# A two-layer transformer on one core: GpSimd in written order, side work at fixed places of a step, head biases picked on chip, routing moved two steps forward

## The chip, the cores and the metric

The kernel runs on one core of one Trainium2 chip. A core has TensorE (PE; its weight loads are shown as PEld), VectorE (DVE), ScalarE (ACT), GpSimd (POOL) and SyncE (SP), which issues most of the DMAs. The metric is the device time of one execution in microseconds (us), the median of several runs. All times below come from one profiled execution unless a median is named.

## The reference, cut to what matters

x is 2 x 1024 x 256 (two batches, 16 tiles of 128 tokens in all), the context 2 x 77 x 256, all in f32. Four sub-layers follow one another; each normalizes the rows (LN) and adds its result to x.

```python
x = x + xattn(LN(x), ctx, ctx, mask, Wq, bq, Wk, bk, Wv, bv, Wo, bo)  # 16 heads of 16, 77 keys
x = x + heads(LN(x), Wq, bq, Wk, bk, Wv, bv, Wr, br, Wo, bo)          # 4 of 16 heads of 64, 1024 keys
x = x + einsum(gelu(einsum(LN(x), ctx)), ctx)                         # 77 context rows as a hidden layer
x = x + moe(LN(x), w_router, w1, b1, w2, b2)                          # top 1 of 8 experts, hidden 1024

def heads(y, ...):
    dist = softmax(mean(y @ Wr + br, axis=1))       # one choice for a whole batch
    idx  = sort(top_k(dist, 4))
    Q, K, V = the idx heads of y @ Wq + bq, y @ Wk + bk, y @ Wv + bv
    return softmax(Q @ K.T / 8) @ V, heads side by side, @ Wo + bo
```

So the second attention can't project anything until the mean over all 1024 tokens of its batch is known, and the experts need the router's choice for every token.

## The kernel before

The program has three phases.

**Phase a**, steps a0 to a19, one tile of 128 tokens a step, software-pipelined: step s makes the scores of tile s (`a_scores`), transposes the weights of tile s-1 (`a_transposed`), forms the weights of tile s (`a_weights`: row maximum and subtraction on DVE, exponential on ACT), multiplies tile s-2 with the values (`a_values`; `rc` and `hn` normalize it on DVE), turns tile s-3 and projects tile s-4 (`a_projected`, which adds to `xs`, the residual stream in SBUF). Before step a0 stand the turned weights of q and k, the keys (`context_k`, laid out by head in `kblk`) and the first queries. The values are spread over heads by `context_v` and `place_v`.

**Phase b**, steps b0 to b36, is the second attention. An item is one tile with two of the four heads, 32 items. Step s makes the scores of item s (`b_scores`, tile `bsc`), transposes the weights of item s-1 in four groups of four (`b_transposed(j, h, k0)`, tiles `bpt` to `beT`), takes row maxima and exponentials of item s (`b_weights`, `bnm` and `be`), multiplies item s-3 with v (`b_values`, `bov`), and every second step forms the reciprocal sums, turns them (`b_inverse_sums`, `b_turned_sums`: `brb`, `brt`, `brT`) and normalizes (`b_normalized`, `boT`). `b_projected` (`po_b`) adds to `xs`.

**Phase e**, from about 500 us, sorts tokens by expert and runs 20 blocks of 128 tokens through the experts' weights; the change does not touch it.

Work that belongs to other sub-layers is hung on these steps as side pieces:

- `do_rows(tag, t0)` normalizes the rows of two tiles: statistics on DVE, the power -1/2 and the two rows `y` on POOL (on DVE for the last two tiles of c and d), then on POOL the next output bias into `xs`. `do_turn` transposes them on PE and ACT copies them to `yT`. The tag is a for the first attention, b for the second, c for the context layer, d for the experts' router.
- `route_sums`, `route_logits`, `route_heads` choose the four heads of a batch; `route_heads` then has SP read each head's number and load its slices of Wk, Wq, Wv and of the biases. `b_qk` projects q and k, `b_v` the values.
- `c_hidden`, `c_out`, `d_logits`, `d_expert` are the context layer and the router for two tiles; groups g = 0 to 7 follow four steps apart.

The order of the work is written by hand for PE, DVE and ACT: these three run their instructions as the program text lists them. POOL's order was left to the framework's scheduler. `at(stage, s, f, ...)` hangs a piece on a step and `take` runs the pieces after the step's own work; only one projection a step goes in the middle (`project`). The weights of the chosen heads have one buffer each, so those of batch 1 wait for the projections of batch 0. PSUM is split into three pools: `big` (scores, two tiles of two banks), `trp` (transposes, two banks) and `accp` (accumulation, two banks).

Of the kernel before, what the change touches and what calls it, by code (L numbers as in the profile page):

```python
# [39 lines left out]
def kernel(  # L40
# [127 lines left out]
    nc.sync.dma_start(wrt_s, w_router.rearrange("(c p) e -> p c e", p=P))  # L168
    b1r = const.tile([E * FC, P], F32, name="b1r")
# [176 lines left out]
    def context_k(m, eng):  # L346
        ps = accp.tile([P, B, KC], F32, name=f"kps_{m}", tag="acc")
        for c in range(C):
            nc.tensor.matmul(
                ps.rearrange("p b k -> p (b k)"),  # L350
                lhsT=wT["k"][:, c, m * P : (m + 1) * P],
                rhs=ctxT[:, c].rearrange("p b k -> p (b k)"),
                start=(c == 0),
                stop=(c == C - 1),
            )
        kT = small.tile([P, B, KC], F32, name=f"kT_{m}", tag="kT")
        nc.vector.scalar_tensor_tensor(kT, ps, bk_c[:, m : m + 1], keep01, ALU.add, ALU.mult)
        for j in range(HG):
            eng.tensor_scalar(kblk[:, :, m, j, :], kT, hmask[:, j : j + 1], None, ALU.mult)
# [10 lines left out]

    def context_v(b):
        ps = accp.tile([KC, D], F32, name=f"vcps_{b}", tag="acc")
# [4 lines left out]
        nc.vector.tensor_tensor(vc[:, b, :], ps, bv_b[:KC, :], ALU.add)  # L377

    def place_v(g):
        ps = accp.tile([P, half, B, HW, HD], F32, name=f"vps_{g}", tag="acc")  # L380
        for i in range(half):
# [3 lines left out]
                ps[:, i].rearrange("p b h d -> p b (h d)"),  # L385
# [3 lines left out]
            )  # L389
        gs = slice(g * half, (g + 1) * half)  # L390
# [94 lines left out]
    def a_step(s):  # L485

        scs = a_scores(s) if s < T else None
        if 0 <= s - 1 < T:
            a_transposed(s - 1, 0, nc.scalar.copy)
            a_transposed(s - 1, 4, nc.scalar.copy)  # L490
        if s < T:
            a_weights(s, scs)
        if 0 <= s - 2 < T:
            a_values(s - 2)
# [5 lines left out]
        if 0 <= s - 4 < T:  # L500
            a_projected(s - 4)

# [4 lines left out]
    def route_sums(b, n):  # L507

        if b not in sel:
            sel[b] = small.tile([P, 2, C], F32, name=f"ys_{b}", tag="ysum")  # L510
        nc.vector.tensor_reduce(
            sel[b][:, n // 512, :], yTs["b", b][:, :, n : n + 512], AX.X, ALU.add
        )

    def route_logits(b):
        ys = sel[b]
        ym = small.tile([P, C, P], F32, name=f"ym_{b}", tag="ym")
        nc.vector.tensor_tensor(ys[:, 0, :], ys[:, 0, :], ys[:, 1, :], ALU.add)
        nc.vector.tensor_scalar(
            ym, ys[:, 0, :].unsqueeze(2).to_broadcast([P, C, P]), 1.0 / S, None, ALU.mult  # L520
        )
        ps = sel[b] = accp.tile([P, NH], F32, name=f"rps_{b}", tag="acc")
# [10 lines left out]
    def route_heads(b):  # L533
# [31 lines left out]
        bc = {k: wsp.tile([P, NP], F32, name=f"bc_{k}{b}", tag=f"bc_{k}") for k in "qk"}  # L565
        bv = wsp.tile([P, NA, FD], F32, name=f"bvs_{b}", tag="bvs")
        for s in range(NA):
            h = nc.values_load(seli[0:1, s : s + 1], engines=SP, min_val=0, max_val=NH - 1)
            for k, src in (("k", f_wk), ("q", f_wq), ("v", f_wv)):
                v = src.rearrange("(c p) (h d) -> p c h d", p=P, h=NH)  # L570
                nc.sync.dma_start(w[k][:, :, s : s + 1, :], v[:, :, bass.ds(h, 1), :])
            with nc.allow_non_contiguous_dma(reason="bias columns"):
                for k, src in (("k", f_bk), ("q", f_bq)):
                    v = src.rearrange("(h d) -> d h", h=NH)
                    r = slice((s % 2) * FD, (s % 2) * FD + FD)
                    nc.sync.dma_start(bc[k][r, s // 2 : s // 2 + 1], v[:, bass.ds(h, 1)])
            v = f_bv.rearrange("(h d) -> h d", h=NH)
            nc.sync.dma_start(bv[:, s, :], v[bass.ds(h, 1), :].to_broadcast([P, FD]))

        bqs = wsp.tile([P, NP], F32, name=f"bqs_{b}", tag="bqs")  # L580
        nc.gpsimd.tensor_scalar(bqs, bc["q"], float(FD) ** -0.5, None, ALU.mult)
        sel[b] = w, {"k": bc["k"], "q": bqs}, bv
# [133 lines left out]
    def b_step(s, project=None):  # L716

# [3 lines left out]
        sc = b_scores(i) if i < NI else None  # L721
        if 0 <= j < NI:
# [5 lines left out]
        if project is not None:  # L728
            b_qk(*project)()
# [8 lines left out]
        if 0 <= k < NI:  # L738
            if k % TG == 0:
                b_turned_sums(k // TG)  # L740
            else:
                b_normalized(k // TG)
        i = s - PR
        if 0 <= i < NI and split(i)[2] == NP - 1:
            b_projected(i)

# [3 lines left out]
    def c_hidden(t0):  # L750

# [3 lines left out]
        for c in range(C):  # L755
            nc.tensor.matmul(
                ps, lhsT=ctxT[:, c, b, :], rhs=yT[:, c, :], start=(c == 0), stop=(c == C - 1)
            )
        g = gs[t0] = ap_.tile([KC, 2 * P], F32, name=f"g_{t0}", tag="g")
# [30 lines left out]
    TE2 = [P, 2, E]  # L790

    def d_logits(t0):
        yT = yTs.pop(("d", t0))
        ps = trp.tile([P, 2, E], F32, name=f"elps_{t0}", tag="tr")
# [6 lines left out]
        nc.vector.tensor_copy(logits[:, t0 : t0 + 2, :], ps)  # L801

    def d_expert(t0):

        ts_ = slice(t0, t0 + 2)
        lg, hot = logits[:, ts_, :], oh[:, ts_, :]
# [28 lines left out]
    def at(stage, s, f, *args):  # L835
        plan.setdefault((stage, s), []).append((f, args))

    def take(stage, s):
        for f, args in plan.pop((stage, s), []):
# [21 lines left out]
    at("a", 0, turn_weight, "v")  # L861
    for b in range(B):
        at("a", 0, context_v, b)
    at("a", 0, do_rows, "a", 4, bo_b)
    at("a", 0, do_rows, "a", 6, bo_b)
    at("a", 0, add_bias, 0, 4, bo_b)
    for g in range(2):
        at("a", 1, place_v, g)
    at("a", 1, do_turn, "a", 4)
    at("a", 1, do_turn, "a", 6)  # L870
    at("a", 1, do_rows, "a", 8, bo_b)
    at("a", 2, query, 0, 512, 0)
    at("a", 2, query, 0, 512, 1)
    at("a", 3, turn_weight, "o")
    at("a", 3, do_turn, "a", 8)
    at("a", 3, do_rows, "a", 10, bo_b)
    at("a", 4, do_turn, "a", 10)
    at("a", 4, do_rows, "a", 12, bo_b)
    at("a", 5, do_turn, "a", 12)
    at("a", 5, query, 1, 0, 0)  # L880
    at("a", 6, query, 1, 0, 1)
    at("a", 6, do_rows, "a", 14, bo_b)
    at("a", 7, do_turn, "a", 14)
    at("a", 8, query, 1, 512, 0)
    at("a", 9, query, 1, 512, 1)
    at("a", 10, expert_biases)

    for i in range(4):
        at("a", 2 * i + 6, do_rows, "b", 2 * i, fbo_b)
        at("a", 2 * i + 7, do_turn, "b", 2 * i)  # L890
    at("a", 10, route_sums, 0, 0)
    at("a", 14, route_sums, 0, 512)
    at("a", 14, route_logits, 0)
    at("a", 15, route_heads, 0)
    for args in ((0, "k", 0, 0), (0, "k", 0, 512)):
        at("a", 17, do_qk, *args)
    at("a", 18, do_qk, 0, "q", 0, 0)
    for s, args in ((0, (0, "k", 1, 0)), (0, (0, "k", 1, 512)), (1, (0, "q", 1, 0))):
        at("b", s, do_qk, *args)
    for t in range(NT):  # L900
        at("b", (0, 0, 1, 1, 2, 2, 3, 3)[t], b_v, 0, t)

    for i in range(4):
        s = 2 * i + 14
        stage, s = ("a", s) if s < 19 else ("b", s - 19)
        at(stage, s, do_rows, "b", NT + 2 * i, fbo_b)
        s = 2 * i + 15
        stage, s = ("a", s) if s < 19 else ("b", s - 19)
        at(stage, s, do_turn, "b", NT + 2 * i)
    at("b", 0, route_sums, 1, 0)  # L910
    at("b", 3, route_sums, 1, 512)
    at("b", 3, route_logits, 1)
    at("b", 4, route_heads, 1)
    project = {4: (0, "q", 0, 512), 5: (0, "q", 1, 512)}
    for s, args in enumerate(
        (("k", 0, 0), ("k", 0, 512), ("q", 0, 0), ("k", 1, 0), ("k", 1, 512), ("q", 1, 0),
         ("q", 0, 512), ("q", 1, 512))
    ):
        project[s + 7] = (1, *args)
    for t in range(NT):  # L920
        at("b", 10 + t, b_v, 1, t)

    for g in range(T // TG):
        s, t0 = 4 * g, TG * g
        at("b", s + 8, do_rows, "c", t0, None, None, g == T // TG - 1)
        at("b", s + 10, do_turn, "c", t0, accp, "acc")
        at("b", s + 12, c_hidden, t0)
        at("b", s + 13, c_out, t0)
        at("b", s + 13, do_rows, "d", t0, None, ztok, g == T // TG - 1)
        at("b", s + 14, do_turn, "d", t0, accp, "acc")  # L930
        at("b", s + 16, d_logits, t0)
        at("b", s + 16, d_expert, t0)
    at("b", 30, d_probability, 0, NT)

    with tc.manual_schedule(
        engines={mybir.EngineType.PE, mybir.EngineType.DVE, mybir.EngineType.Activation}
# [15 lines left out]
        rows["a", 0], rows["a", 2] = ys[:2], ys[2:]  # L952
        for b in range(B):
# [8 lines left out]
        context_k(0, nc.vector)  # L962
        context_k(1, nc.gpsimd)
        for j in range(HG):
            nc.vector.tensor_scalar(
                mneg[:, :, j, :], mask_i, 0.0, neg3, ALU.is_equal, ALU.mult
            )
        query(0, 0, 0)
        query(0, 0, 1)
        for s in range(T + 2):  # L970
            a_step(s)
            take("a", s)
# [3 lines left out]
        take("a", T + 2)  # L976
        for s in range(NI + PR):
            b_step(s, project.get(s))
# [232 lines left out]
```

## Time and profile before

| | |
|---|---|
| median of 3 runs | 679.14 us (676.03 to 679.31) |
| profiled execution | 681.69 us, of which its span 679.9 us |
| busy in the span | PE 592.3 (87%), PEld 430.8 (63%), DVE 340.1 (50%), ACT 236.5 (35%), POOL 172.4 (25%) |
| mean granted TensorE clock | 0.93 |
| moved by DMA | 62.72 MB, most of it the experts' weights after 500 us |

The page is read so: busy time counts an engine's instructions, and matmul ends are modelled. The slices cut the span in 40 parts of 17 us; a digit is the busy share in tenths, and PEclk is the TensorE clock that was granted. A list of waits says which instruction of which engine stood idle, what released it, the total, how often and the longest. A group's line has its line in the program, engine, operation, the tile written and those read, shapes and count, then busy time and the mean of one. The scores of step a2 begin at 40.42 us in this execution, those of b0 at 173.25, and the last product with v ends at 460.27.

### The profile page before, as it was taken

How to read it: one execution, taken by the hardware profiler on the slowest of the kernel's cores; microseconds unless marked ns; L12 is line 12 of the kernel's file. 1: busy time of each engine (PE TensorE's matmuls, PEld its weight loads, DVE VectorE, ACT ScalarE, POOL GpSimd, SP SyncE). 2: the span in 40 equal slices, each digit the busy share in tenths (PEclk: the TensorE clock that was granted, in tenths of full speed). 3: DMA queues.
4: the chain of work that ended last, by engine and by line, in shares of the span. 5: the costliest groups of instructions: out<-in, count | busy, mean ns of one | idle time of the engine just before them, and what ended most of it. 6: DMA issues, size and time to landing. Idle time of an engine off the chain costs nothing. (4 is left out here: it accounts for less than half of the span.)

```text
span 679.9 us, 9956 instructions
## 1 busy us (share of the span) xinstructions
PE 592.3 (87%) x3661; PEld 430.8 (63%) x3661; DVE 340.1 (50%) x824; ACT 236.5 (35%) x473; POOL 172.4 (25%) x218
## 2 busy tenths in 40 slices
PE   6689999987888999999999999995444999999995
PEld 3368777875454555565655566563334999899884
DVE  4457666752355655464767675763360332332331
ACT  3235454531244444434444645531100211111110
POOL 3363352223120002021222130303122122323121
PEclk9679999969798999999999999998555999999999
DMA  8000000002000100000000000000129499999990
GB/s 241 1 1 1 1 1 1 1 1 53 3 0 1 39 17 1 1 16 16 1 32 16 16 21 11 33 1 31 47 101 358 175 341 353 361 354 373 331 321 15
DMA packets 50824, 62.72 MB, mean 92 GB/s; under 512 B 12664, under 2 KB 43859, under 8 KB 50773
## 3 DMA queue, kind: packets, MB, share of 16 engines
q1 hardware_dynamic: 47504, 54.03, 23.7%
q0 software_dynamic: 2560, 7.34, 3.0%
q10 hardware_dynamic: 709, 0.68, 0.3%
q8 instruction: 30, 0.49, 0.3%
q14 instruction: 21, 0.17, 0.1%
HBM read 55.75 MB, written 6.82 MB: 92 GB/s over the span
## 5 line engine op out<-in xcount | busy, mean ns | idle before, releaser
L654 DVE TENSOR_REDUCE bnm<-bsc 128x1 f32<-128x1024 f32 x64 | 75.3, 1219 | 45.0 <-PE bsc L640 45.0
L666 PEld LDWEIGHTS bpt<-ident,be 128*128 128x128 f32 x512 | 54.8, 141 | 43.6 <-issue 20.4
L656 ACT ACTIVATE be<-bsc,bnm 128x1024 f32<-128x1024 f32 x64 | 70.8, 1110 | 17.1 <-DVE bnm L654 16.1
L666 PE MATMUL bpt<-ident,be 128*128 128x128 f32 x512 | 71.4, 280 | 5.8 <-DVE beT L667 5.3
L1131 PE MATMUL ph<-ybT,w1s 128*128 128x128 f32 x640 | 76.3, 278 | 0.0
L1131 PEld LDWEIGHTS ph<-ybT,w1s 128*128 128x128 f32 x640 | 74.5, 195 | 2.6 <-DVE ybT L1126 2.2
L1148 PE MATMUL epo<-w2s,ehT 128*128 128x256 f32 x320 | 75.2, 379 | 0.0
L1137 ACT ACTIVATE ehT<-ph,b1s 128x128 f32<-128x128 f32 x80 | 22.9, 369 | 144.8 <-issue 105.7
L640 PE MATMUL bsc<-kT,qT 64*128 64x512 f32 x256 | 67.1, 644 | 5.8 <-ACT qT L598 5.8
L667 ACT COPY beT<-bpt 128x512 f32<-128x512 f32 x64 | 37.5, 586 | 95.8 <-PE bpt L666 94.8
L1139 DVE TENSOR_SCALAR ehT<-ph,b1s 128x128 f32<-128x128 f32 x80 | 22.5, 345 | 93.8 <-ACT ehT L1137 88.9
L676 PE MATMUL bov<-beT,v 128*64 128x256 f32 x512 | 62.3, 385 | 0.0
L1148 PEld LDWEIGHTS epo<-w2s,ehT 128*128 128x128 f32 x320 | 57.9, 190 | 6.3
L667 DVE COPY beT<-bpt 128x512 f32<-128x512 f32 x64 | 43.4, 686 | 29.3 <-PE bpt L666 29.2
L676 PEld LDWEIGHTS bov<-beT,v 128*64 128x64 f32 x512 | 33.9, 136 | 25.5 <-issue 7.4
L688 POOL COPY brb<-brc 128x256 f32<-128x256 f32 x16 | 6.4, 400 | 153.6 <-DVE brc L686 150.4
L640 PEld LDWEIGHTS bsc<-kT,qT 64*128 64x128 f32 x256 | 23.0, 194 | 31.0 <-issue 21.9
L1157 POOL DMA_INDIRECT out_dram<-ob,etok x20 | 20.2, 1012 | 82.5 <-DMA out_dram<-ob,etok 70.0
L456 PE MATMUL av<-vblk,eT 128*128 128x51 f32 x320 | 39.6, 282 | 0.0
L456 PEld LDWEIGHTS av<-vblk,eT 128*128 128x128 f32 x320 | 39.6, 202 | 0.1
L432 DVE TENSOR_REDUCE mx<-sc 128x8 f32<-128x616 f32 x32 | 25.4, 794 | 26.3 <-PE sc L418 26.3
L448 ACT COPY eT<-pt 128x512 f32<-128x512 f32 (+1 forms) x48 | 23.3, 514 | 38.1 <-PE pt L447 37.5
(227 smaller groups left out, 849.7 us busy)
## 6 DMA issues: line engine op xcount, KB each, us to landing
w1s<-in_L_ffn_w_dram SPq DMA_DIRECT2D x20, 1024.0 KB
w2s<-in_L_ffn_w_dram SPq DMA_DIRECT2D x20, 1024.0 KB
b2s<-in_L_ffn_b_dram SPq DMA_DIRECT2D x20, 128.0 KB
xs<-in_x_dram SPq DMA_DIRECT2D x4, 512.0 KB
ztok<-xs SPq DMA_DIRECT2D x16, 128.0 KB
ztok<-y_d SPq DMA_DIRECT2D x16, 128.0 KB
ws_k<-in_L_ffn_Wk_dram SPq DMA_DIRECT2D x8, 64.0 KB
ws_q<-in_L_ffn_Wq_dram SPq DMA_DIRECT2D x8, 64.0 KB
```

The source lines that it names most:

```text
L432: nc.vector.tensor_reduce(mx, scv, AX.X, ALU.max)
L448: copy(eTs[t][:, c0 : c0 + n, :], pt[:, :n, :])
L456: nc.tensor.matmul(av[:, h0 : h0 + HW, :].rearrange("p h d -> p (h d)"), lhsT=eT[:, c, :], rhs=vblk[:, t // NT, c].rearrange("p h d -> p ( ...
L640: nc.tensor.matmul(sc[h][:, n : n + 512], lhsT=qks[b, "q", m][r, q0 : q0 + P], rhs=qks[b, "k", m][r, n : n + 512], start=True, stop=True,)
L654: nc.vector.tensor_reduce(nm, sc[h], AX.X, ALU.max, negate=True)
L656: nc.scalar.activation(bes[i][:, h], sc[h], AF.Exp, bias=nm, accum_out=sms[g][:, q, s : s + 1])
L666: nc.tensor.transpose(pt[:, k - k0, :], bes[i][:, h, k * P : (k + 1) * P], ident)
L667: copy(beTs[gm][:, h, k0 : k0 + 4, q * P : (q + 1) * P], pt)
L676: nc.tensor.matmul(ovs[gm][h * FD : (h + 1) * FD, :], lhsT=vs[g * TG // NT][:, k, 2 * m + h, :], rhs=beTs[gm][:, h, k, :], start=(k == 0), ...
L1131: nc.tensor.matmul(ph[:, f, :], lhsT=ws[n][0][:, c, f * P : (f + 1) * P], rhs=ybT[:, c, :], start=(c == 0), stop=(c == C - 1),)
L1137: nc.scalar.activation(hT[:, f, :], ph[:, f, :], AF.Relu, bias=b1s[:, f : f + 1])
L1148: nc.tensor.matmul(po, lhsT=hT[:, f, :], rhs=w2s[:, f, :], start=(f == 0), stop=(f == FC - 1))
```

## The change

- POOL's instructions also run in written order. The second half of `kblk` is formed on DVE, not POOL. Rows 4 to 7 of phase a are normalized ahead of the context's transposes, W_v is turned ahead of step a0, and the bias of tiles 0 to 7 is one piece at the end of a0.
- `at` and `take` get a position inside a step: 0 after the scores, 1 (phase a) after the weights, 2 (phase b) after the first two groups of transposes, 3 at the end. Producers in PSUM and their readers are split (`context_v` and `context_v_bias`, `place_v` and `place_v_heads`, `c_hidden` and `c_gelu`; `d_logits` leaves its copy to `d_expert` and uses `accp`). The turned sums go from the end of the odd step to just behind the scores of the next step.
- The biases of all 16 heads of q and k are loaded once, turned on PE (`head_biases`), and the chosen ones are picked on DVE with a one-hot product. The loads of columns and the small POOL operation on q's bias are gone. SP loads k and q slices first, then v, then v's biases.
- The routing of batch 0 sums two tiles at a time, forms its mean in a13 and its heads in the middle of a14 (before: a14 and the end of a15). The projections start at the end of a15 (before: a17). Batch 1 has logits and heads in b3 (before: b3 and b4).
- The context layer and router of group g run from 4g+8 to 4g+13 instead of 4g+8 to 4g+16.

```diff
+    hbr = const.tile([2 * NH, 2, FD], F32, name="hbr")
+    for i, ap in enumerate((f_bk, f_bq)):
+        for j in range(2):
+            nc.sync.dma_start(hbr[i * NH : (i + 1) * NH, j, :], ap.rearrange("(h d) -> h d", h=NH))
...
         for j in range(HG):
-            eng.tensor_scalar(kblk[:, :, m, j, :], kT, hmask[:, j : j + 1], None, ALU.mult)
+            nc.vector.tensor_scalar(kblk[:, :, m, j, :], kT, hmask[:, j : j + 1], None, ALU.mult)
...
+    def head_biases():
+
+        ps = trp.tile([P, 2 * NH], F32, name="hbps", tag="tr")
+        nc.tensor.transpose(ps, hbr.rearrange("p j d -> p (j d)"), ident[: 2 * NH, : 2 * NH])
+        nc.scalar.copy(hbT[:, 0, :], ps[:, :NH])
+        nc.scalar.activation(hbT[:, 1, :], ps[:, NH:], AF.Copy, scale=float(FD) ** -0.5)
...
+    def route_mean(b):
+        ys = small.tile([P, C], F32, name=f"yt_{b}", tag="yt")
+        nc.vector.tensor_reduce(ys, sel[b], AX.X, ALU.add)
+        ym = sel[b] = small.tile([P, C, P], F32, name=f"ym_{b}", tag="ym", bufs=1)
+        nc.vector.tensor_scalar(
+            ym, ys.unsqueeze(2).to_broadcast([P, C, P]), 1.0 / S, None, ALU.mult
+        )
...
+        load(0, "k", "q")
+        load(1, "k", "q")
+        load(2, "k")
+        load(3, "k", "q")
+        load(2, "q")
         for s in range(NA):
-            h = nc.values_load(seli[0:1, s : s + 1], engines=SP, min_val=0, max_val=NH - 1)
-            for k, src in (("k", f_wk), ("q", f_wq), ("v", f_wv)):
...
-                    nc.sync.dma_start(bc[k][r, s // 2 : s // 2 + 1], v[:, bass.ds(h, 1)])
...
-        nc.gpsimd.tensor_scalar(bqs, bc["q"], float(FD) ** -0.5, None, ALU.mult)
+            load(s, "v")
...
+        hot = small.tile([P, NA, NH], F32, name=f"hot_{b}", tag="hot", bufs=1)
+        nc.vector.tensor_tensor(
+            hot, iota16.unsqueeze(1).to_broadcast([P, NA, NH]),
+            se.unsqueeze(2).to_broadcast([P, NA, NH]), ALU.is_equal,
+        )
+        hb = small.tile([P, 2, NA, NH], F32, name=f"hb_{b}", tag="hb", bufs=1)
+        nc.vector.tensor_tensor(
+            hb, hot.unsqueeze(1).to_broadcast([P, 2, NA, NH]),
+            hbT.unsqueeze(2).to_broadcast([P, 2, NA, NH]), ALU.mult,
+        )
...
         sc = b_scores(i) if i < NI else None
+        take("b", s, 0)
+        if 0 <= k < NI and k % TG == TG - 1:
+            b_turned_sums(k // TG)
         if 0 <= j < NI:
             b_transposed(j, 0, 0, nc.scalar.copy)
         if i < NI:
             b_weights(i, sc)
         if 0 <= j < NI:
             b_transposed(j, 0, 4, nc.vector.tensor_copy)
-        if project is not None:
-            b_qk(*project)()
+        take("b", s, 2)
...
-        if 0 <= k < NI:
-            if k % TG == 0:
-                b_turned_sums(k // TG)
-            else:
-                b_normalized(k // TG)
+        if 0 <= k < NI and k % TG == TG - 1:
+            b_normalized(k // TG)
         i = s - PR
         if 0 <= i < NI and split(i)[2] == NP - 1:
             b_projected(i)
+        take("b", s, 3)
...
+    at("a", 0, 3, add_bias, 0, 8, bo_b)
...
+    at("a", 13, 3, route_logits, 0)
+    at("a", 14, 1, route_heads, 0)
+    at("b", 3, 2, route_logits, 1)
+    at("b", 3, 3, route_heads, 1)
...
     for t in range(NT):
-        at("b", 10 + t, b_v, 1, t)
+        at("b", 8 + t, 0, b_v, 1, t)
...
-        at("b", s + 8, do_rows, "c", t0, None, None, g == T // TG - 1)
-        at("b", s + 10, do_turn, "c", t0, accp, "acc")
-        at("b", s + 12, c_hidden, t0)
-        at("b", s + 13, c_out, t0)
-        at("b", s + 13, do_rows, "d", t0, None, ztok, g == T // TG - 1)
-        at("b", s + 14, do_turn, "d", t0, accp, "acc")
-        at("b", s + 16, d_logits, t0)
-        at("b", s + 16, d_expert, t0)
-    at("b", 30, d_probability, 0, NT)
+        at("b", s + 8, 3, do_rows, "c", t0, None, None, last)
+        at("b", s + 10, 0, do_turn, "c", t0)
+        at("b", s + 10, 2, c_hidden, t0)
+        at("b", s + 10, 3, c_gelu, t0)
+        at("b", s + 11, 2, c_out, t0)
+        at("b", s + 11, 3, do_rows, "d", t0, None, ztok, last)
+        at("b", s + 12, 2, do_turn, "d", t0, accp, "acc")
+        at("b", s + 13, 2, d_logits, t0)
+        at("b", s + 13, 3, d_expert, t0)
+    at("b", 30, 3, d_probability, 0, NT)
...
-        context_k(0, nc.vector)
-        context_k(1, nc.gpsimd)
+        context_k(0)
...
+        context_k(1)
         query(0, 0, 0)
         query(0, 0, 1)
+        turn_weight("v")
         for s in range(T + 2):
             a_step(s)
```

In the last loop s stands for 4g and t0 for 2g; the same loop of before has no positions.

## Prediction

> **What bounds the kernel now.** I read the page's slices first, then TensorE's waits, the windows with their clocks, and the timeline at each long wait.
>
> ```profile
> PE   6689999987888999999999999995444999999995
> ...
> PEclk9679999969798999999999999998555999999999
> ```
> A slice is 17 us. TensorE (PE) is full in the middle of both attentions and in the experts (527 us to the end). It has holes at the start, around slices 8 to 12, and at the seam (slices 27 to 30); the clock dips in the same places.
>
> ```profile
> PE bsc L640 <- ACT qT L598: 5.8, 1, 5.8
> ...
> PE sc L409 <- POOL kblk L359: 4.5, 1, 4.5
> PE lps_a L306 <- POOL y_a L283: 2.4, 2, 1.7
> PE bpt L666 <- DVE beT L667: 2.3, 2, 1.2
> PE rps L524 <- issue: 2.2, 1, 2.2
> PE rps L524 <- DVE ym L519: 2.2, 1, 2.2
> PE vcps L374 <- ACT wvT L337: 1.9, 1, 1.9
> PE bps_k L591 <- DMA ws_k<-in_L_ffn_Wk_dram: 1.5, 1, 1.5
> ```
> TensorE's waits up to 222 us (total, times, longest): single events, nearly all at a step that the change moves.
>
> ```profile
> 21.80:32.00 10.20, 8.29 (x28) 4.47 (x30) 3.81 (x10) 1.19 (x2) 0.10 (x1) 0.50 0.00 1
> ...
> 38.80:45.70 6.90, 6.18 (x28) 4.12 (x27) 3.40 (x5) 1.58 (x3) 6.59 (x6) 0.51 0.00 1
> ...
> 141.30:151.50 10.20, 10.20 (x47) 9.53 (x44) 5.26 (x15) 3.76 (x7) 4.42 (x4) 0.50 0.01 2
> ...
> 172.00:178.80 6.80, 5.55 (x12) 2.70 (x13) 1.73 (x2) 1.16 (x2) 0.48 (x2) 0.50 0.01 2
> ...
> 222.00:440.00 218.00, 208.85 (x1296) 126.28 (x1295) 135.43 (x265) 108.92 (x198) 40.05 (x47) 1.00 0.06 17
> ```
> Windows: length, busy time of PE, PEld, DVE, ACT, POOL, then the granted clock. After each long wait the clock is halved for 7 to 10 us, so a wait costs itself and half the busy time that follows. 222 to 440 us (the body of the second attention) is full: 9.15 us idle in 218.
>
> The Trainium skill ("TensorE: Matmul & The Clock Gate", "Why this matters for your kernels") asks only that idle gaps stay below about 3 us. The trace disagrees: after a gap of 2.21 us (at 139.35) the window from 141.3 is at 0.50. By the page, the short gaps below would cost no clock and the sum would be some 7 us smaller.
>
> **The change, part by part** (gains positive, us).
>
> *Start, +13.* POOL first adds bo_b (16.72 to 19.05, having waited for the load), only then forms half of kblk (4 operations, 2.67), for which PE waits 4.5. On DVE the like four took 0.93, and DVE's queue becomes: y_a to 10.15, row statistics of four more tiles (2.45, as at 30.45 to 32.9), keep01 0.23, kT and kblk 1.3, mneg 0.92, kT and kblk 1.3: ready at 16.4. PE ends the queries at 16.4 and now turns W_v there (1.1), so the first scores begin near 17.5 and end near 19; the v projection follows without its 1.9 wait (3.70 at half clock, some 1.9 at full). DVE ends step 0's weights and the v bias at 22.4, place_v (2.4) then runs to 24.8, the transposes of e to 26.4, two turned blocks to 28. Their rows are ready, since POOL makes them from 11.4 to 17.7, ahead of the 4.7 us of bias adds (eight tiles in one; nothing needs those before step 4). Step 2's scores stood at 40.42: 12.4 sooner, and half of the slow 5.3 us after it is 2.6 more. I take 13 because holes of 1 to 1.5 us remain in steps 0 and 1; bounds 9 and 16 (all waits, 8.8, plus half of 8.29 and 6.18).
>
> *First routing, +5.8.* It now sums per two tiles and forms the mean inside step 13, behind the weights; rps no longer waits: 2.2 and half of 10.2. Against it: DVE carries, in steps 13 to 15, 4.3 us of standing work each, rows (1.35) twice, sums and mean 1.7, logits 0.35, the head choice 2.3, and the bias pick, for which no row stands: three operations on 64 to 128 elements by the nearest rows (0.22 to 0.29) and two copies, 1.2 or so. That is 21.2 us against PE's 21.3: no cover left. What queues behind it on DVE is rc and hn, then the step's residual add, then the next step's row maxima; PE meets them as late PSUM buffers. I charge 1.5; bounds 0 to 7.3.
>
> *Heads' weights, +9.9.* SP issued six loads a head, some 3.7 us, two of them columns of 4-byte elements; q's bias came last and passed POOL:
>
> ```profile
> 172.24 0.24 POOL L581 TENSOR_SCALAR bqs<-bc_q 128x2 f32<-128x2 f32 x1
> 172.51 0.69 ACT L598 ACTIVATE qT<-bps_q,bqs 128x512 f32<-128x512 f32 x1 [6.78 <-POOL bqs L581]
> ...
> 173.25 3.79 PE L640 MATMUL bsc<-kT,qT 64*128 64x512 f32 x8 [5.76 <-ACT qT L598]
> ```
> Now the bias never leaves the chip and k of head 1 is SP's third load, not its seventh: issued about 10.5 us after step 14 begins, landing 2 to 2.4 later (158.17 to 160.59 before), while PE wants it at about 14. Gone: 1.5, 5.8, half of the 5.55 slow us after 173.25 (2.8), and the 2.8 of bpt waits behind it: 12.9. But k, q and v projections have moved ahead, so steps b0 to b2 have less to fill the chain scores 2.0, row maxima 2.35, exponentials 1.3 (5.9 with hand-overs; 7.3 where v's bias add stands ahead of the maxima) and wait 3.0 in all. Bounds 5 and 12.9. The four extra bias loads (0.5 each on SP) stand ahead of b1r alone, which step 11 wants. In batch 1, q's first load holds SP until the last q projection of batch 0, at the end of b5; k of head 1 lands about 4 us later, wanted a step (8 us) later.
>
> *Second routing, +3.9.* The 2.2 wait and half of the 3.5 slow us after it; bounds 1 and 3.9.
>
> *Body of the second attention, -6.4.* Putting the turned sums behind the scores frees the buffer waits (the 9.15). But the router's turned block moves from a step's end to its position 2, one step after its rows are begun. A step of the same kind as it stands:
>
> ```profile
> 435.89 1.09 PE L666 MATMUL bpt<-ident,be 128*128 128x128 f32 x8
> ...
> 436.34 0.71 POOL L279 TENSOR_TENSOR rs_d<-rs_d,minus_half 128x2 f32<-128x2 f32 x1 [3.83 <-DVE rs_d L278]
> ...
> 437.16 2.43 POOL L283 TENSOR_SCALAR y_d<-xs,mv_d,rs_d 128x256 f32<-128x256 f32 x2
> ...
> 439.72 0.60 PE L306 MATMUL lps_d<-ident,y_d 128*128 128x128 f32 x4
> ```
> Position 2 is where the first bpt end, 436.9; y_d ends at 439.59. In the new order: residual add 0.5 after the step's end, statistics 1.4, power 0.8, y 1.25 each: 5.25, against scores 2.0, turned sums 0.4 and transposes 1.1, PE there at 3.5. Less its own 0.6, PE stands 1.5 in each of five groups and 3.5 in the sixth, whose step has no scores: 11. The context's turned block takes a transpose buffer, and the next transposes wait for its copy (0.59 less 0.41 covered, with hand-overs 0.45) seven times: 3. v's projections at position 0: 0.2 eight times. 9.15 - 15.6 = -6.4; bounds -15 and +9.
>
> *Seam, +5.5.* From the last bov (460.27) to the last logits (near 497.7) now 37.4. Group 6's context goes before that point, so its router rows end 9.0 after it, the last projection 9.9, group 7's y 13.5, its gelu 19.4, its output 21.3 and its logits 28.6, each step at the timeline's price (y_d of group 6 still on POOL, 2.43). That is 8.8 less; but 3.2 us of PE work has moved ahead of the point. Bounds 2 and 9. From there on nothing changes.
>
> Sum: 13 + 5.8 + 9.9 + 3.9 - 6.4 + 5.5 = 31.7, and 0.9 for two stray waits on rows in the first attention (0.77 and 1.10): 32.6. The profiled execution took 681.69 (span 679.9), 2.55 above the median of 679.14: it would take 649.1, the median 646.5; I say 646.
>
> A page speaks against moving kblk: the Trainium skill ("Perfetto Trace Analysis", "Optimizing Scalar/DVE Operations") warns that shifting work between GpSimd and VectorE may not help, as they share a port. The trace has 0.93 on one and 2.67 on the other for the same four operations; by the page up to 1.7 us would be lost.
>
> **Rivals.** *The body does not stand* (0.20): if y comes in time for position 2, the 14 of turned blocks vanish: 632. For: today lps_d starts without a wait. Against: the place is 2.7 us sooner than y's end.
> *The clock does not recover* (0.15): the holes left in steps 0, 1 and 13 to 15 halve it again. A gap of 1.9 preceded a slow stretch, one of 1.5 did not. Price: half of 8.29, of 6.18 and of 10.2, 12.3 and the holes' own 2: 660.
> *DVE sets the step* (0.07, slower): v's add, the context's and the router's small operations now stand ahead of the row maxima in a b step. A step is 7.8, the chain 5.9: 1.9 of slack. Beyond it each us of DVE delay lengthens the step; 3.2 late in all 32 steps costs 42 and gives 688. It outdoes the gain from 2.9 late. The trace says 1.4 in eight steps, under 1 elsewhere.
> *It comes to nothing* (0.04): the order on POOL was not what delayed the start, and later stalls eat the routing: 677 to 681.
>
> **How the numbers follow.** The forecast has 0.54 (640 to 654 by its own errors). Range 630 to 664: the forecast, the first rival nearly whole and the second; outside lie the last two rivals and the edges. A measurement of this kernel tells 0.5% (3.4 us) from no change. Faster 0.89, same 0.04, slower 0.07.
>
> **What would show it.** Scores of step 2 near 28; no wait of sc on kblk; bsc without its 5.8; clock 1.00 from 30 to 440; new waits of lps_d on POOL's y_d, 1.5 each, in the body; the last logits some 29 after the last bov. Wrong would be: no lps_d waits, or clock 0.50 near 140, or DVE near full from 170 to 440.

## The result, and the profile after

| | before | changed |
|---|---|---|
| median | 678.59 us (676.03 to 679.31) | 660.86 us (659.47 to 662.67) |
| profiled execution | 681.69, span 679.9 | 659.47, span 657.7 |
| mean granted clock | 0.930 | 0.946 |

The ratio is 0.975 (95% interval 0.971 to 0.978), four runs of each: faster by 17.7 us where 32.6 were forecast. The time lies within the range, near its slow end. Between the two profiled executions the difference is 22.2 us.

The slices of the changed kernel, of 16.4 us each:

```profile
PE   5999999898899999999989999875455999999995
...
PEclk9999999999899999999989999985556999999999
```

Counted from 0 as in the prediction, the holes of slices 8 to 12 are mostly filled (two slices are at 8), and the clock is whole until the seam, but for two slices at 0.8. The seam itself (here slices 26 to 30) is still there.

TensorE's waits up to 199 us, where step b6 begins (total, times, longest):

```profile
PE wps_q L339 <- DMA raw_q<-in_L_xattn_Wq_dram: 5.2, 1, 5.2
PE bpt L719 <- DVE beT L720: 3.2, 2, 1.6
PE wps_k L339 <- ACT ctxT L1017: 1.3, 1, 1.3
PE lps_a L311 <- ACT eT L460: 1.2, 2, 0.9
PE bps_k L644 <- PE po_a L492: 0.9, 1, 0.9
```

Of the waits that the prediction showed, those of `sc` on `kblk`, `bsc` on `qT`, `rps` on `ym`, `vcps` on `wvT`, `lps_a` on POOL and `bps_k` on its load are gone. Those of `bpt` remain, 3.2 instead of 2.3, and now stand in steps b1 and b2. From 199 to 475 us, the last logits, they read:

```profile
PE lps_d L311 <- POOL y_d L288: 13.2, 13, 3.9
PE gpo L825 <- DVE g L819: 3.8, 2, 1.9
PE lps_d L311 <- DVE y_d L288: 3.4, 1, 3.4
PE bpt L719 <- ACT yT_c L312: 2.1, 6, 0.5
PE lps_c L311 <- POOL y_c L288: 1.8, 2, 1.1
PE lps_c L311 <- DVE y_c L288: 1.5, 1, 1.5
```

This is the wait that the prediction named, TensorE turning the router's rows before POOL has made them, and it is the longest item of the list. The kernel before had it too; from 231 to 498 us its line reads:

```profile
PE lps_d L306 <- POOL y_d L283: 10.7, 4, 5.8
```

All of these 10.7 us stand behind the last `bov`. In the changed kernel 5.4 stand in the body, 3.4 in the short steps (those from b31 to the last `bov`, of which only b31 has scores) and 4.4 behind the last `bov`. The two traces cut at the same work give the table below; the three stages from b6 to the last logits are also shown as windows (length, busy PE, PEld, DVE, ACT, POOL, granted clock, DMA share, GB/s).

| from the start to | before | changed | gained so far |
|---|---|---|---|
| scores of a2 | 40.4 | 29.8 | 10.6 |
| scores of a4 | 57.8 | 44.7 | 13.1 |
| scores of a15 | 139.9 | 122.2 | 17.7 |
| scores of b6 | 230.6 | 198.5 | 32.1 |
| scores of b31 | 441.3 | 416.4 | 24.9 |
| end of the last `bov` | 460.3 | 444.4 | 15.9 |
| end of the last logits | 497.7 | 475.1 | 22.6 |
| end | 679.9 | 657.7 | 22.2 |

Before:

```profile
230.60:441.30 210.70, 201.59 (x1255) 122.47 (x1254) 129.90 (x249) 105.27 (x191) 40.04 (x47) 1.00 0.06 17
441.30:460.30 19.00, 18.53 (x133) 12.28 (x132) 11.70 (x32) 6.93 (x14) 2.02 (x3) 1.00 0.02 5
460.30:497.70 37.40, 18.56 (x68) 13.13 (x68) 12.27 (x47) 4.52 (x9) 9.18 (x10) 0.66 0.12 41
```

Changed:

```profile
198.50:416.40 217.90, 206.80 (x1267) 124.69 (x1266) 129.61 (x254) 104.80 (x192) 39.28 (x45) 0.99 0.06 17
416.40:444.40 28.00, 22.34 (x141) 13.76 (x140) 12.50 (x37) 8.29 (x17) 7.08 (x8) 0.94 0.06 20
444.40:475.10 30.70, 16.09 (x50) 11.09 (x48) 10.61 (x36) 2.97 (x6) 4.54 (x5) 0.54 0.10 35
```

So 32.1 us were won by b6, 7.2 given back in the body and another 9.0 in the short steps from b31 to the last `bov`, of which the rest of the seam returned 6.7.

In the changed kernel's timeline, the two places that gave most back (start, duration; in brackets the idle time before):

```profile
424.31 1.28 PE L719 MATMUL bpt<-ident,be 128*128 128x128 f32 x8
...
426.90 2.43 POOL L288 TENSOR_SCALAR y_d<-xs,mv_d,rs_d 128x256 f32<-128x256 f32 x2
...
428.18 0.44 PE L311 MATMUL lps_d<-ident,y_d 128*128 128x128 f32 x2 [2.59 <-POOL y_d L288]
...
429.38 0.44 PE L311 MATMUL lps_d<-ident,y_d 128*128 128x128 f32 x2 [0.76 <-POOL y_d L288]
...
452.35 2.43 POOL L288 TENSOR_SCALAR y_d<-xs,mv_d,rs_d 128x256 f32<-128x256 f32 x2
...
453.62 0.69 PE L311 MATMUL lps_d<-ident,y_d 128*128 128x128 f32 x2 [3.92 <-POOL y_d L288]
...
455.31 1.91 PE L761 MATMUL po_b<-fwo_s,boT 128*128 128x256 f32 x4
...
457.26 0.42 DVE L765 TENSOR_TENSOR xs<-po_b,xs 128x256 f32<-128x256 f32 x1 [5.81 <-PE po_b L761]
```

At 428 a step without scores reaches the turned block after its transposes and stands for 2.59 and 0.76. At 453.6 the turned block of group 6 stands at position 2, *ahead of* the last projection (`po_b`), which needs nothing of POOL. TensorE takes its queue in written order, so the projection, the residual add at 457.26 and all of group 7 behind it waited for two rows of another group.

### The profile page after: what moved, and what is told of

The parts are those of the page before. It is cut to its first block, busy times and chain, and to the rows that moved or that the text cites. A ratio compares the mean times of both kernels' runs of the same rounds, so it can differ in the third digit from the quotient of the medians.

```text
span 657.7 us, 9891 instructions
## 1 busy us (share of the span) xinstructions
PE 585.8 (89%) x3662; PEld 425.2 (65%) x3662; DVE 342.9 (52%) x842; ACT 234.5 (36%) x475; POOL 168.8 (26%) x210
## 4 chain that ended last, share of the span: by engine, by line
PE 75%; DVE 7%; POOL 6%; issue 4%; ACT 2%; DMA 2%; POOLq 0%; ACTq 0%; DVEq 0%
PE ph L1190 11%; PE epo L1207 10%; PE bov L729 9%; PE bpt L719 8%; PE bsc L693 8%; PE av L468 4%; PE sc L421 3%; POOL y_d L288 3%; PE vbps L662 2%; PE po_b L761 2%; PE pt L459 2%; DMA zb<-ztok,etok 2%; PE qps L323 2%; PE po_a L492 1%; PE gpo L825 1%
## 5 line engine op out<-in xcount | busy, mean ns | idle before, releaser
L719 PE MATMUL bpt<-ident,be 128*128 128x128 f32 x512 | 72.8, 281 | 6.6 <-DVE beT L720 3.2
L719 PEld LDWEIGHTS bpt<-ident,be 128*128 128x128 f32 x512 | 55.6, 141 | 33.6 <-issue 10.2
L709 ACT ACTIVATE be<-bsc,bnm 128x1024 f32<-128x1024 f32 x64 | 70.8, 1111 | 10.4 <-DVE bnm L707 9.8
L729 PE MATMUL bov<-beT,v 128*64 128x256 f32 x512 | 65.6, 401 | 1.5 <-ACT qT L651 1.5
L693 PE MATMUL bsc<-kT,qT 64*128 64x512 f32 x256 | 64.9, 618 | 0.0
L729 PEld LDWEIGHTS bov<-beT,v 128*64 128x64 f32 x512 | 35.2, 141 | 25.4 <-issue 9.9
L468 PE MATMUL av<-vblk,eT 128*128 128x51 f32 x320 | 37.4, 272 | 0.9 <-DVE hn L476 0.9
L468 PEld LDWEIGHTS av<-vblk,eT 128*128 128x128 f32 x320 | 37.1, 192 | 1.6 <-DVE hn L476 1.1
L444 DVE TENSOR_REDUCE mx<-sc 128x8 f32<-128x616 f32 x32 | 25.4, 793 | 16.4 <-PE sc L430 16.4
```

What stands on the lines that cost most here:

```text
L444: nc.vector.tensor_reduce(mx, scv, AX.X, ALU.max)
L468: nc.tensor.matmul(av[:, h0 : h0 + HW, :].rearrange("p h d -> p (h d)"), lhsT=eT[:, c, :], rhs=vblk[:, t // NT, c].rearrange("p h d -> p ( ...
L693: nc.tensor.matmul(sc[h][:, n : n + 512], lhsT=qks[b, "q", m][r, q0 : q0 + P], rhs=qks[b, "k", m][r, n : n + 512], start=True, stop=True,)
L709: nc.scalar.activation(bes[i][:, h], sc[h], AF.Exp, bias=nm, accum_out=sms[g][:, q, s : s + 1])
L719: nc.tensor.transpose(pt[:, k - k0, :], bes[i][:, h, k * P : (k + 1) * P], ident)
L729: nc.tensor.matmul(ovs[gm][h * FD : (h + 1) * FD, :], lhsT=vs[g * TG // NT][:, k, 2 * m + h, :], rhs=beTs[gm][:, h, k, :], start=(k == 0), ...
```

## The experiments

The theory going in was that the mechanism of the prediction holds, and that the router's turned block costs most in the short steps. Rivals were POOL's written order, the clock, and the routing's load on DVE. Medians of before were 678.8, 677.5 and 680.6 us in the three groups of runs; each ratio is to the runs of before beside it.

**e1: POOL left to the scheduler again.**

```diff
-            mybir.EngineType.Pool,
```

> The changed kernel with POOL's order left to the scheduler again; kblk stays on DVE, all else as changed. Theory (the start's gain comes from kblk on DVE and from rows 4 to 7 being begun early, the written order only keeps POOL from delaying them): POOL may put the bias adds (4.7 us from 16.7) ahead of the rows of tiles 4 to 7, which then end near 27, about when PE turns them in a1; 0 to 2 us lost, 660 to 663 us. Rival (the written order itself carries the start): most of the 13 us is lost, 669 to 674 us, and the turned blocks of a1 wait for POOL's y_a.

663.11 us (660.22 to 667.59), ratio 0.977 (0.973 to 0.981). Steps a2 and a15 begin at 29.8 and 122.2, as in the changed kernel, b0 at 153.4 instead of 152.8. The written order on POOL neither makes the gain nor takes it back; what it is worth (2 us by the medians) is inside the intervals.

**e2: the router's turned block at the end of its step.**

```diff
-        at("b", s + 12, 2, do_turn, "d", t0, accp, "acc")
+        at("b", s + 12, 3, do_turn, "d", t0, accp, "acc")
```

> The changed kernel with the router's turned block at position 3 of its step instead of 2. Theory (the block stands ahead of its own rows): PE's waits of lps_d on POOL's y_d in the body, 1.3 us in each of four steps and 3.4 in the one without scores, are gone, and in step 36 the last projection no longer stands behind y_d of group 6 (4.4): 8 to 13 us less than the changed kernel, 648 to 653 us. Rival (the step is set by row maxima and exponentials, and the waits only stand in for them): other waits of PE take their place, under 3 us less, 658 to 661 us.

644.28 us (643.50 to 645.71), ratio 0.951 (0.949 to 0.954): 16.6 us less than the changed kernel for one digit, more than the 8 to 13 expected. TensorE's waits from 199 to 458 us in e2:

```profile
PE gpo L825 <- DVE g L819: 3.8, 2, 1.9
PE lps_d L311 <- DVE y_d L288: 3.4, 1, 3.4
PE lps_d L311 <- POOL y_d L288: 3.0, 2, 2.2
PE bpt L719 <- ACT yT_c L312: 2.1, 6, 0.5
```

The waits on POOL fall from 13.2 to 3.0, and the stages follow (windows of e2):

```profile
198.70:408.30 209.60, 203.96 (x1268) 124.11 (x1267) 129.63 (x254) 105.02 (x192) 39.39 (x45) 1.00 0.06 18
408.30:430.50 22.20, 20.44 (x141) 13.10 (x140) 12.52 (x37) 8.30 (x17) 7.05 (x8) 1.00 0.07 25
430.50:457.80 27.30, 14.98 (x48) 10.25 (x48) 10.72 (x37) 2.97 (x6) 4.52 (x5) 0.62 0.12 39
```

Body 8.3 shorter, short steps 5.8, seam 3.4. The waits removed are 10.2 of these 17.5; another 5.8 is busy time of TensorE, as the clock goes with the waits (0.94 to 1.00 in the short steps, 0.54 to 0.62 in the seam). The body of e2 is also 1.1 shorter than that of before, though more work stands in it: but for this one, the written places cost the body nothing in this pair of traces.

**e3: the kernel before, with the second half of `kblk` on DVE.**

```diff
-        context_k(1, nc.gpsimd)
+        context_k(1, nc.vector)
```

> The kernel before with one edit: the second half of kblk on DVE. Theory: PE's wait of 4.5 us for kblk goes and half of the slow-clock stretch from 21.8 with it, 5 to 9 us less than before, 670 to 674 us; the rows of tiles 4 to 7 still come late (2.4). Rival (another wait stood right behind it): the W_v copy and the rows take the time back, at most 2 us, 677 to 679 us.

673.36 us (670.64 to 676.93), ratio 0.991 (0.988 to 0.995): 5.4 us of the start come from this line alone; a2 begins at 35.1 instead of 40.4. The other 5.3 of the changed kernel's 10.6 there are the rest of the start's new order, which was not taken apart.

**e4: the kernel before, with the biases picked on chip and the loads in order of need,** routing in its old steps.

```diff
+        load(0, "k", "q")
+        load(1, "k", "q")
...
-                    nc.sync.dma_start(bc[k][r, s // 2 : s // 2 + 1], v[:, bass.ds(h, 1)])
...
+        nc.vector.tensor_tensor(
+            hot, iota16.unsqueeze(1).to_broadcast([P, NA, NH]),
...
-        nc.gpsimd.tensor_scalar(bqs, bc["q"], float(FD) ** -0.5, None, ALU.mult)
```

> The kernel before with the head biases picked on chip and the heads' weights loaded in order of need, routing and schedule as before. Theory: bsc's wait of 5.8 us on qT goes with the 2.8 of slow clock behind it, and the wait of 1.5 on ws_k: 7 to 10 us less than before, 669 to 672 us. Rival (the loads of k and q are late anyway without the earlier routing): PE waits for the weights instead, at most 3 us less, 675 to 679 us.

670.78 us (669.06 to 672.39), ratio 0.990 (0.987 to 0.993): 8.0 us for both together; how they share it was not taken apart. Two of TensorE's waits up to 215 us in e4:

```profile
PE rps L537 <- DVE ym L532: 4.4, 2, 2.3
...
PE bsc L678 <- ACT qT L636: 0.8, 1, 0.8
```

`bsc` falls from 5.8 to 0.8 and the wait for k's weights is gone; the wait of the routing stays, as it should.

**e5: the changed kernel, with batch 0's routing in its old steps** (mean and logits in a14, heads at the end of a15, projections from a17).

```diff
...
-    at("a", 13, 3, route_logits, 0)
-    at("a", 14, 1, route_heads, 0)
+    at("a", 14, 3, route_logits, 0)
+    at("a", 15, 3, route_heads, 0)
...
```

> The changed kernel with batch 0's routing back at its old places: rows, turns and sums one step later, mean and logits at the end of a14, heads at the end of a15, projections from a17 on, v's from b0 on. Biases and loads stay as changed. Theory (forecast's step on the first routing): rps waits for the mean again, 2.2 us, and the clock is halved behind it, 1.7 to 5.1; part comes back because steps b0 to b2 have more to fill them: 2 to 6 us more than the changed kernel, 663 to 667 us. Rival (with the biases on chip the earlier routing buys nothing): 659 to 662 us.

664.08 us (659.69 to 665.23), ratio 0.977 (0.970 to 0.985), 3.2 above the changed kernel by the medians but with an interval that holds it. By the trace b6 begins at 203.0 instead of 198.5, and 1.0 of this stands ahead of a2 already, where a load came later. The old 2.2 wait did not come back: `rps` waits 0.5, probably because the sums over two tiles leave less for the end. What came were a wait of `av` on `hn` (1.9, where the changed kernel has 0.9) and half the clock from 137.8 to 144.6. So the sooner routing is worth 3.2 us by the medians and 3.5 by these traces, which the runs do not tell from nothing, and in the trace not through the wait that was priced.

The remaining runs start from e2 and ask what holds it.

**e6: rows of group 6 on DVE too.**

```diff
-        at("b", s + 8, 3, do_rows, "c", t0, None, None, last)
+        at("b", s + 8, 3, do_rows, "c", t0, None, None, g >= T // TG - 2)
...
-        at("b", s + 11, 3, do_rows, "d", t0, None, ztok, last)
+        at("b", s + 11, 3, do_rows, "d", t0, None, ztok, g >= T // TG - 2)
```

> e2_turn_end (644.3 us) with the rows y of group 6, context and router, on DVE instead of POOL, as group 7's already are. Theory (the seam is a chain through POOL's 2.43 us of y): lps_c of group 6 no longer waits (0.6), lps_d of group 6 saves most of 2.2 and 0.8: 2 to 4 us less, 640 to 642 us. Rival (group 7's own chain ends last and DVE, now with 1.6 us more, delays it): 0 to 1 us less, 643 to 645 us.

642.55 us (640.21 to 644.28), ratio 0.948 (0.941 to 0.955). By the trace, b31 to the last logits takes 46.5 instead of 49.5. The medians can't be told from e2's.

**e7: idle transposes in the seam's holes,** 66 in phase b and 42 ahead of the router's probabilities and the sorting.

```diff
...
+    for s, pos, n in ((35, 2, 10), (36, 3, 14), (38, 0, 4), (38, 2, 4), (39, 2, 10), (40, 2, 20), (41, 2, 4)):
+        at("b", s, pos, warm, n)
...
```

> e2_turn_end (644.3 us) with idle transposes of the identity on PE in the seam's holes (10 ahead of gpo, 14 ahead of lps_d, 20 ahead of the last lps_d and so on, 46 ahead of the sorting); nothing reads them. Theory (the seam runs at half clock from 440 us on because of its holes, and that halves the chain's own matmuls): clock near 1.00 up to the sorting's matmuls, half of some 17 us of PE work, 5 to 8 us less: 636 to 639 us. Rival (the chain runs through DVE and POOL, PE's share is small, or the clock falls all the same): under 2 us less, or more than 644 us where the idle transposes stand in the way.

642.23 us (640.15 to 643.65), ratio 0.948 (0.941 to 0.955), again not separable from e2. The windows of e7, last `bov` to last logits and from there to the experts:

```profile
432.70:458.10 25.40, 19.90 (x117) 16.35 (x117) 10.61 (x36) 2.97 (x6) 4.50 (x5) 0.87 0.12 42
458.10:484.10 26.00, 13.49 (x82) 12.38 (x81) 10.99 (x46) 0.26 (x1) 7.03 (x10) 0.66 0.74 255
```

The clock rises from 0.62 to 0.87 in the first, but its length falls only from 27.3 to 25.4, and the second from 26.5 to 26.0. In this run, then, little of the seam's chain is TensorE's time: what sets it are rows, gelu and adds on the other engines. Half the clock is a sign of the seam here, hardly its cause; whether the idle transposes themselves held up a link is not shown.

**e8: the context's turned block in the accumulators' PSUM, two q projections at a step's end.**

```diff
-        at("b", s + 10, 0, do_turn, "c", t0)
+        at("b", s + 10, 0, do_turn, "c", t0, accp, "acc")
...
-        (9, 3, ("k", 1, 512)), (10, 3, ("q", 1, 0)), (17, 2, ("q", 0, 512)), (21, 2, ("q", 1, 512)),
+        (9, 3, ("k", 1, 512)), (10, 3, ("q", 1, 0)), (17, 3, ("q", 0, 512)), (21, 3, ("q", 1, 512)),
```

> e2_turn_end (644.3 us) with the context's turned block in an accumulation bank instead of a transpose bank, and batch 1's last two q projections at the end of steps b17 and b21 instead of position 2. Theory (single waits for PSUM buffers): the waits of bpt on yT_c's copy (0.46, seven times in body and seam) and of bov on qT (0.75, twice) are gone: 3 to 5 us less, 639 to 641 us. Rival (an accumulation bank is then short): other waits of the same size, 643 to 645 us.

643.14 us (639.22 to 643.79), ratio 0.947 (0.940 to 0.954). In the body the waits of `bpt` on `yT_c` (2.1) and of `bov` on `qT` (1.5) are gone, and two of `bps_q` on the logits' copy (0.5 each) and six of `bpt` on `brT` (1.6 in all) are new; b6 to b31 takes 208.5 instead of 209.6, and b31 to the last logits 50.3 instead of 49.5. The medians show no difference.

**e10: two v projections at the ends of b1 and b2** instead of behind their scores.

```diff
-             ("b", 1, 0), ("b", 1, 3), ("b", 2, 0), ("b", 2, 3))[t], b_v, 0, t)
+             ("b", 1, 3), ("b", 1, 3), ("b", 2, 3), ("b", 2, 3))[t], b_v, 0, t)
```

> e2_turn_end (644.3 us) with batch 0's value projections of steps b1 and b2 at the end of the step instead of one of them at position 0. Theory (at position 0 v's bias add stands on DVE ahead of the row maxima and of the copy that frees a transpose buffer): PE's waits of bpt on beT, 1.6 us in b1 and in b2, are gone and the clock stays up behind them: 3 to 4 us less, 640 to 641 us, steps b1 to b6 shorter by that. Rival (steps b1 and b2 are short of PE work and wait for the exponentials anyway): the waits move to the scores, under 1 us less.

641.46 us (639.08 to 645.02), ratio 0.941 (0.937 to 0.945). TensorE's waits from 150 to 200 us:

```profile
PE bpt L719 <- DVE beT L720: 1.8, 2, 1.2
PE bpt L719 <- ACT beT L720: 0.5, 2, 0.2
```

The two waits of 1.6 in the changed kernel and e2 become 0.65 and 1.19, and two of 0.24 on ACT's copies are new. From b1 to b6 it takes 38.2, where e2 takes 41.2; but e8, whose code in these steps is that of e2 and which has both waits of 1.6, takes 39.6. Between e2 and e8 lies one half-clock stretch, 174.2 to 177.6 in e2, none in e8. So 1.4 is the edit's own; the other 1.6 is the clock that e2 happened to lose and e8 did not. The v projections behind the scores, whose bias adds stand on DVE ahead of the row maxima, made part of the `bpt` waits (3.2 in all, 2.3 without them). The interval lies below e2's (0.949 to 0.954), but the two were timed in different groups of runs; by the medians e10 is 2.8 us less.

**e9: e2, e6, e7, e8 and e10 together.**

> All of e2_turn_end, e6_seam_dve, e7_warm, e8_body and e10_v_end together. Theory (separate waits, the gains of the profiled parts add: seam rows 2, clock 2, buffer waits 3, v's adds 3): 10 us less than e2_turn_end, 634 us, between 632 and 637. Rival (the same microseconds counted twice, since seam and clock overlap): 638 to 641 us.

632.76 us (630.58 to 636.51), ratio 0.931 (0.926 to 0.935), faster than both kernels: 28 below the changed one by the medians. Each of the four small edits was within or near the noise by itself; together they take 11.5 us from e2's median, where the stretches named above gave 3.0, 2.4, 1.1 and 3.0, in all 9.5 (the 1.1 without e8's loss behind b31, the last 3.0 with the half clock of e2). The slices of e9, of 15.7 us:

```profile
PE   5999999999899999999999999998739999999995
...
PEclk9999999989999999999999999998968999999999
```

The seam's hole, five slices in the changed kernel, is two here (7 and 3). From the last `bov` to the last logits it takes 22.4 us (changed 30.7, before 37.4).

## Why the prediction was right, and where it was too high

- **Start (13 forecast).** Right: 13.1 by a4. Step 2's scores stood at 29.8, not 28; the rest came in steps 2 and 3, as the half-speed stretch after them went.
- **First routing (5.8, with 0.9 for stray waits).** 4.6 between a4 and a15: the wait of 2.2 is gone, and so are the stray waits, which came to 2.2 there (0.35, 0.77 and 1.10 of `lps_b`) and not to 0.9. The other terms lie behind a15. The lack of DVE cover came as charged (1.5): `av` waits 0.85 for `hn` at 125.6, and `bps_k` 0.92 until 130.30, when DVE has read the buffer of `av` that it takes (`hn`, to 130.19). Half of the 10.2 was had between these two traces, where the changed kernel is at 1.00 until 173.8. For the medians it was too much: in e3 and e4 the same wait is followed by 3.4 us at half clock (from 134.1 and 139.0), so that half of 3.4 is what another execution would lose.
- **Heads' weights and second routing (9.9 and 3.9).** With the clock share of the first routing (5.1) and the charge for DVE (1.5), 17.4 were forecast between a15 and b6, and 14.4 came. TensorE's idle time fell by 7.4 there where the terms make 7.8. Its busy time fell by 7.0 where the shares of the clock make 9.6: 1.7 of the difference is a half-clock stretch of the changed kernel's own (173.8 to 177.2, behind the second wait of 1.6), the rest is not explained. e4 shows 8.0 for the weights and biases without the sooner routing. Steps b0 to b2 were charged 3.0 of waiting and have 3.2.
- **Body (-6.4).** The mechanism was right. A group was charged 1.5 and four of them have 0.52 and 0.76, 1.3 (a fifth has 0.32); the step without scores was charged 3.5 and has 3.35; the context's turned block was charged 0.45 and has up to 0.5, six times. From b6 to b31 the loss is 7.2, where the terms that lie there came to 5.3: 6.4 without the sixth group's 3.5, and with 2.4 of context work that moved into the stretch (PE is busy 203.96 there in e2, 201.59 before). The missing 1.9 are mostly a stretch of half clock from 330.8, 1.7, behind one of the 1.3 waits; three like it were followed by none.
- **Seam (+5.5).** This step failed. Counted from b31, with the sixth group's wait and the moved work, it should have gained 5.5 - 3.5 + 2.4 = 4.4, and it lost 2.3. Of these 6.7, 4.7 lie ahead of the last `bov`: the short steps were to lose the 3.5 and 0.8 of moved work, and lost 9.0. What was not priced is that in steps without scores `y_c` comes late as well (1.05 and 0.77), that the wait of 2.59 is followed by 3.4 us at half clock (429.8 to 433.2, 1.7), and that more work had moved (in e2, at full clock, PE is busy 20.44 there, before 18.53). The other 2.1 lie in the chain behind that point, priced link by link at 28.6: it takes 30.7. Group 6's rows end 10.3 after the last `bov`, not 9.0, and the last projection 12.8, not 9.9, for the turned block's second tile and the projection itself run at half clock behind the rows. The prediction had the projection behind the rows, but did not ask whether it must stand there: in e2, where it stands ahead, it ends 6.2 after the last `bov` and the chain takes 27.3. Of what e2 gains on the changed kernel, 9.2 lie behind b31.
- **Phase e (0).** 0.4 longer.

These misses make the 10.4 us between the sum of 32.6 and the 22.2 of the profiled executions: 1.4 up to b6 (0.1 more than forecast by a4 and 1.5 more by a15, then 3.0 less by b6), 1.9, 6.7 and 0.4. The other 4.5 up to the 17.7 of the medians come from the choice of the trace as the base. The profiled execution of before was 3.1 us above its median, with half-clock stretches at the start and behind `rps` that were longer than those of e3 and e4 (below), and the one of the changed kernel 1.4 below its own. The prediction took 2.55 of that off the time, but still priced the gain from the long stretches.

That the time lies within the range is in part luck. Its slow end was set for a rival, **the clock does not recover**, whose 660 is nearly the measured time, and that rival did not come: the changed kernel is at 1.00 through phase a (e6, e7 and e9, with the same code there, each have one half-clock stretch of 3.4 from 128 to 132). One of its reasons was misread: the gap of 1.9 stands inside a slow stretch (at 26.4, in 21.8 to 32.0), and the stretch from 38.8 follows one of 1.70. **The body does not stand** fell (5.4 us of waits on `y_d` in the body). **DVE sets the step** did not come: DVE is busy 129.61 of 217.9 us in the body, and the chain of b1 and b2 is the one place where its order showed. **It comes to nothing** fell with the interval.

Still open: the value of the sooner routing to better than a few us (e5's interval is 0.970 to 0.985), how much of the second routing's share is its own, and which part of the start's new order made the other half of its gain.

## What to carry to other kernels

On an engine that runs in written order, a consumer placed before its input is made holds everything behind it; price such a place in the shortest step that it occurs in, not in the usual one, and ask what independent work stands behind it. Here one place cost 16.6 of 660.9 us. When a trace is priced, take only that part of a half-clock stretch that other executions of the same code would show too.

## What the runs showed of the hardware

The same wait is followed by half-clock stretches of different lengths. Behind the first 2.2 us of `rps` it was 10.2 us in the profiled execution of before and 3.4 in e3 and in e4, whose code is the same up to there but for edits that do not bear on that step. Behind the second, 2.17 in batch 1, it was 3.4 in before and in e4, and in e3 there was none. The windows of e4, two at the start and the one behind `rps`:

```profile
22.90:29.70 6.80, 4.78 (x14) 2.62 (x15) 2.18 (x4) 1.19 (x2) 0.00 (x0) 0.50 0.01 1
36.60:43.40 6.80, 4.92 (x20) 2.74 (x21) 3.57 (x10) 1.23 (x3) 6.53 (x6) 0.50 0.00 1
139.00:142.40 3.40, 3.40 (x16) 1.96 (x15) 3.16 (x10) 0.40 (x2) 1.60 (x2) 0.50 0.00 0
```

All lengths seen ahead of the end of a run are close to 3.4 us or its multiples. So are the distances between their starts: in before the stretches that the prediction shows begin at 21.8, 38.8, 141.3 and 172.0, which lie 5, 30 and 9 times 3.413 us apart, and in the changed kernel at 173.8, 330.8, 429.8 and 446.8, which lie 46, 29 and 5 times 3.413 apart. The Trainium skill ("TensorE: Matmul & The Clock Gate", "What's actually happening") states a free-running activity window of 3413 ns, which the lengths and the distances agree with; that the stretches differ between executions would fit it, but no run here shows how much idle time in a window brings one on. Waits shorter than the window are enough: in the changed kernel, after 0.52 and 0.76 a stretch came once of four times. The two waits of 1.6 in b1 and b2 stand in seven traces (changed, e1, e2, e5 to e8) and were followed by one 8 times of 14: both times in e1, e6 and e7, once in the changed kernel and e2, not at all in e5 and e8.
